# Layernorm results turned features first by transposing DMAs of 16-bit halves, in a transformer tower with routed experts on one core

## The chip, the cores and the metric

The kernel runs on 1 core of one Trainium2 chip. The metric is the device time of one execution in microseconds; the kernel before took 2347.92 us, the median of 3 runs (2347.41 to 2347.99).

The engines are TensorE (PE, with its weight loads PEld), VectorE (DVE), ScalarE (ACT), GpSimd (POOL) and SyncE (SP), which issues most DMAs. Each engine works through its own list of instructions in order and waits for others at semaphores.

## The reference, cut to what matters

The input is cut into patches, Fourier transformed along the patch and embedded: 16384 tokens of D = 256 features, in 4 sequences. Then one layer follows, in float32:

```python
h  = tok(x)                                   # (4, 4096, 256)
z  = layernorm(h)                             # no gain, no bias
a  = layernorm(z) * ln1_g + ln1_b
q, k, v = a@Wq.T + bq, a@Wk.T + bk, a@Wv.T + bv
z1 = z + q * scan(mem = decay*mem + k*v)      # along the sequence
m  = layernorm(z1) * ln2_g + ln2_b
h  = h + z1 + relu(m@W1.T + b1)@W2.T + b2     # hidden size 1024
t  = layernorm(h)
top 2 of 8 experts per token from softmax(t @ router_w.T), weights made to sum to 1
out = h + t + sum over the two experts of weight * (gelu(t@w1[e] + b1[e]) @ w2[e] + b2[e])
```

## The kernel before

The tokens are taken in NB = 32 blocks of BLK = 512 (TT = 4 groups of 128 tokens). Layernorms need tokens on the partitions ("tokens first": a tile of 128 x 4 x 256), matmuls that contract over features need the features there ("features first": 128 x 2 x 512, since D is KD = 2 groups of 128). So three times a block a layernorm's result is turned. `to_features` (L213) does it with eight PE transposes of 128 x 128 (L217) into two PSUM tiles, and ACT brings each to SBUF: with gain and bias of the layernorm as the factors of an activation (L225), or as a plain copy (L219). The three uses are

- `features1` (L291): `zz` to `hT`, for the attention's q, k and v (`retention`, L295). With `scan=True` the tokens are put in the order of the sequence while ACT copies.
- `features2` (L339): the second `zz` to another `hT`, for the hidden layer (`mlp_in`, L343, eight parts m = 0 to 7; `mlp_out`, L349, two halves).
- `features3` (L388): `tok` to `tokT`, for the router (`logits`, L392, one call for 128 tokens). `choose` (L404) then finds the two experts on DVE, and `place` (L458) counts tokens with PE and DVE and writes each token to its two experts' lists in DRAM (`xbuf`) by eight indirect DMAs from POOL (L479). What is written is `row`, made in `mlp_out`: each token's 256 values as two planes of 16-bit halves, all upper halves and then all lower ones (two ACT copies, L376), and its number (an iota on POOL, L381).

`take` (L525) finds which lists hold full tiles of 256 tokens (four more a block in steady state) and adds them to `tiles`. A slot runs one `expert_step` (L728) if more than 3 tiles wait: it issues the loads of a tile up to four ahead on SP (weights L589, the tokens L596, their shares L599), copies the next tile on ACT (`turn`, L602), and lets PE enter one tile and leave the one before (L608, L625), after which DVE makes `y` (L639 to L646) and POOL adds it to the output with two indirect DMAs (L650). The tokens of a tile already come in features first by a transposing DMA from DRAM: the DMA transposes 2-byte elements, so the planes of halves are turned (`xh`, 256 KB), and two ACT copies put the halves of each float32 together again (L606).

The order on PE, DVE, ACT and SP is that of the program (`tc.manual_schedule`, L752); POOL's is left to the scheduler. Iteration i of the main loop works on three blocks: the new one (embedding, first layernorms, attention), the middle one (hidden layer) and the old one (routing). On PE a steady iteration is: embed part 0 (L262); features2 of the middle block; embed part 1 (L273); features3 of the old; embed part 2; a slot; mlp_in 0 to 3, each followed by one `logits`; a slot and `choose`; mlp_in 4 to 6; features1 of the new; mlp_in 7; `place` and `take`; retention; a slot; mlp_out(0); the residual's transposes (L327); a slot; mlp_out(1). The iterations 0 to 3 have no slot, 4 and 5 only the last two; after the loop's last iteration, which has no new block, the last block's experts are run densely between the remaining tiles. The layernorms' `rstd` is made on POOL (L195 to L200) between its indirect DMAs, and DVE applies it (L204).

Of the kernel before, what the change touches and what calls it, by code (L numbers as in the profile page):

```python
# [12 lines left out]
F32 = mybir.dt.float32  # L13
I32 = mybir.dt.int32
U16 = mybir.dt.uint16
AF = mybir.ActivationFunctionType
ALU = mybir.AluOpType
AX = mybir.AxisListType

P = 128  # L20
# [6 lines left out]
BQ, BK, BV, DEC, G1, B1, G2, B2, MB1, EB1 = 0, 2, 4, 6, 8, 10, 12, 14, 16, 24  # L27
# [3 lines left out]
def vit_tower_kernel(  # L31
# [15 lines left out]
    nc = tc.nc  # L47
    B, NBLK, _, XW = x.shape
    D = wtok.shape[1]
# [3 lines left out]
    KD, KH = D // P, H // P  # L53
    J = STRIDE // 2
    TT = 4
    BLK = TT * P
    U = TT // 2
# [8 lines left out]
    NB = B * NBLK  # L66
    NTOK = NB * BLK
    RW = D + 4
    FIRST, DIFF, SECOND, NUMBER = D, D + 1, D + 2, D + 3


    NS = NB - 1
# [12 lines left out]
    def load_x(i):  # L85
        xb = xpool.tile([P, XW], F32, name="xb")
        nc.sync.dma_start(out=xb, in_=x[i // NBLK, i % NBLK])
        return xb
# [5 lines left out]
    with tc.tile_pool(name="prep", bufs=1) as prep:  # L94
# [4 lines left out]
        for h in range(2):  # L99
            rows = slice(h * C, (h + 1) * C)  # L100
# [21 lines left out]
    vec = const.tile([P, vecs.shape[1]], F32)  # L122
    nc.sync.dma_start(out=vec, in_=vecs)
    wqkv_sb = const.tile([P, 3, KD, D], F32)
    nc.sync.dma_start(out=wqkv_sb, in_=wqkv.rearrange("w (k p) d -> p w k d", p=P))
    w1_sb = const.tile([P, KD, H], F32)
# [41 lines left out]
    one = ctx.enter_context(tc.tile_pool(name="one", bufs=1))  # L168
    two = ctx.enter_context(tc.tile_pool(name="two", bufs=2))
# [7 lines left out]
    p_tm = ctx.enter_context(tc.tile_pool(name="p_tm", bufs=3, space=bass.MemoryType.PSUM))  # L177
    p_sm = ctx.enter_context(tc.tile_pool(name="p_sm", bufs=1, space=bass.MemoryType.PSUM))

    class Norm:  # L180


# [27 lines left out]
                    ALU.mult,  # L210
                )

    def to_features(dst, src, g=None, b=None, scan=False):  # L213
        for k in range(KD):
            ps = p_mm.tile([P, BLK], F32, name="mm")
            for t in range(TT):
                nc.tensor.transpose(ps[:, ts(t, P)], src[:, t, ts(k, P)], ident)  # L217
            if g is None:
                nc.scalar.copy(dst[:, k, :], ps)  # L219
            else:  # L220
                into = dst[:, k, :]
                if scan:
                    into = into.rearrange("p (u q r) -> p u r q", u=U, r=2)
                    ps = ps.rearrange("p (u r q) -> p u r q", u=U, r=2)
                nc.scalar.activation(  # L225
                    into, ps, AF.Identity, bias=vec[:, b + k : b + k + 1], scale=vec[:, g + k : g + k + 1]
                )

    def feature_mm(w, rhs, m):

# [7 lines left out]
    class Block:  # L238
# [14 lines left out]
        def embed(self):  # L253
# [34 lines left out]
            norm.apply(self.zz, self.h, 1)  # L288
            norm.apply(self.z, self.h, 0)

        def features1(self):  # L291
            self.hT = two.tile([P, KD, BLK], F32, name="hT")
            to_features(self.hT, self.zz, G1, B1, scan=True)

        def retention(self, m):  # L295
            if m == 0:
# [24 lines left out]
        def residual(self):  # L321
# [14 lines left out]
            nc.vector.tensor_tensor(self.h, self.h, self.z, ALU.add)  # L336
            nc.vector.tensor_tensor(self.h, self.h, mb2_sb.unsqueeze(1).to_broadcast([P, TT, D]), ALU.add)

        def features2(self):  # L339
            self.hT = two.tile([P, KD, BLK], F32, name="hT")  # L340
            to_features(self.hT, self.zz, G2, B2)

        def mlp_in(self, m):  # L343
            if m == 0:
# [4 lines left out]
        def mlp_out(self, u):  # L349
            if u == 0:  # L350
                self.norm = Norm()
            ps = p_tm.tile([P, 2, D], F32, name="tm")
            for i in range(2):
                for k in range(KH):
                    nc.tensor.matmul(  # L355
                        ps[:, i, :],
                        lhsT=self.aT[:, k, ts(u * 2 + i, P)],
                        rhs=w2_sb[:, k, :],
                        start=k == 0,
                        stop=k == KH - 1,  # L360
                    )
            nc.vector.tensor_tensor(self.h[:, ts(u, 2), :], ps, self.h[:, ts(u, 2), :], ALU.add)  # L362
            for i in range(2):
                self.norm.stats(self.h, u * 2 + i)
            if u == U - 1:
                self.norm.factors()
                self.tok = one.tile([P, TT, D], F32, name="tok")
                self.norm.apply(self.tok, self.h)
                nc.vector.tensor_tensor(self.h, self.h, self.tok, ALU.add)
                if self.i == NS:  # L370
                    return

                self.row = two.tile([P, TT, RW], I32, name="row")
                halves = self.tok.rearrange("p t d -> p (t d)").bitcast(U16).rearrange("p (t d i) -> p t d i", t=TT, i=2)
                for i in range(2):
                    nc.scalar.copy(self.row.bitcast(U16)[:, :, i * D : (i + 1) * D], halves[:, :, :, 1 - i])  # L376

                to = out[ts(self.i, BLK), :].rearrange("(u q r) d -> q u (r d)", q=P, r=2)
                self.stored = nc.sync.dma_start(out=to, in_=self.h.rearrange("p (u r) d -> p u (r d)", r=2))
                unordered("sums", self.stored, ())  # L380
                nc.gpsimd.iota(  # L381
                    self.row[:, :, NUMBER : NUMBER + 1],
                    pattern=[[2 * P, U], [1, 2]],
                    base=self.i * BLK,
                    channel_multiplier=2,
                )

        def features3(self):  # L388
            self.tokT = one.tile([P, KD, BLK], F32, name="tokT")
            to_features(self.tokT, self.tok)  # L390
# [126 lines left out]
    def unordered(name, what, others):  # L517

        tc.declare_no_dep(what.ins, group=name, keep=[o.ins for o in others], reason="rows of their own")
        after(what, others)  # L520
        tc.add_to_no_dep_group(name, what.ins)
# [201 lines left out]
    def advance(what, upto):  # L723
        while at[what] < min(upto, len(tiles)):
            getattr(tiles[at[what]], what)()
            at[what] += 1

    def expert_step():  # L728

        n = at["enter"]  # L730
        advance("load", n + AHEAD)
        advance("turn", n + 2)
        advance("enter", n + 1)
        advance("leave", n)
# [3 lines left out]
    blocks = [Block(i) for i in range(NB)]  # L738
# [3 lines left out]
    def slot():  # L742
        if len(tiles) - at["enter"] > LEFT:
            expert_step()
# [7 lines left out]
    with tc.manual_schedule(engines=MANUAL):  # L752
        xs[1] = load_x(1)
        blocks[0].differences(xs.pop(0))
        for i in range(NB + 1):
            new = blocks[i] if i < NB else None
            mid = blocks[i - 1] if i >= 1 else None
            old = blocks[i - 2] if i >= 2 else None
            embed = new.embed() if new else iter(())
            next(embed, None)  # L760
            if mid:
                mid.features2()
            next(embed, None)
            if old:
                old.features3()
            next(embed, None)
            slot()
            for m in range(KH):
                if mid:
                    mid.mlp_in(m)  # L770
                if old and m < TT:
                    old.logits(m)
                if m == TT - 1:
                    slot()
                    if old:
                        old.choose()
                if new and m == KH - 2:
                    new.features1()
                if not new and m == KH - 3:
                    take(old.i + 1, old, old.place())  # L780
            if old and new:
                take(old.i + 1, old, old.place())
            if i + 1 < NB:
                blocks[i + 1].differences(xs.pop(i + 1))
                if i + 2 < NB:
                    xs[i + 2] = load_x(i + 2)
            if new:
                for m in range(KD):
                    new.retention(m)
            slot()  # L790
            if mid:
                mid.mlp_out(0)
            if new:
                new.residual()
            slot()
            if mid:
                mid.mlp_out(1)

        last = blocks[NS]
        for e in range(E):  # L800
            tiles.insert(len(tiles) - 2 * (E - 1 - e), Expert(e, last))
        expert_step()
        expert_step()
        last.features3()
        for t in range(TT):
            last.logits(t)
        last.choose()
        last.combine()
        while at["leave"] < len(tiles):
            expert_step()  # L810
# [82 lines left out]
```

## Time and profile before

| what | value |
|---|---|
| median of 3 runs | 2347.92 us (2347.41 to 2347.99) |
| profiled execution | 2348.05 us, its span 2346.0 us, mean granted PE clock 0.987 |
| DMA, all kinds | 255.91 MB, mean 109 GB/s |
| DMA queue of SP | 30.9% of 16 engines' span |
| DMA queue of POOL | 16.3% |
| longest waits of PE | 25.9 us for `wsum` at the start, 8.7 us for `xd`, 6.5 us for `zz` (2 times), 6.0 us for `xT` (2), 5.7 us for `tok` (1) |

A timeline row has the start in the span, the time to the end of the last instruction of the row, engine, line, operation, output and inputs, and in brackets how long the engine had been idle and what released it. A group row of the page has count, busy time and mean duration (ns) of one, then idle time before its instructions. Matmul ends are modelled, so consecutive PE rows overlap a little, and the step from one start to the next is the better cost. A float32 matmul is two records.

### The profile page before, as it was taken

The page shows a single profiled execution, that of the slowest core. Times are in us where ns is not written, and L with a number is a line of the kernel's source. Part 1 is how long each engine was busy: PE and PEld are TensorE (multiplying, and loading weights), DVE is VectorE, ACT ScalarE, POOL GpSimd, SP SyncE. Part 2 cuts the span into 40 slices and gives each one's busy share as a digit, 9 for nine tenths or more (in the row PEclk, how much of TensorE's full clock was granted, in tenths as well). Part 3 has the DMA queues.
Part 4 walks back from the last instruction along what each step waited for, and adds up shares of the span by engine and source line. Part 5 has one row for each costly group of instructions (what it writes and reads, how often), then busy time and mean ns, then how long its engine had stood idle before and what let it go on. Part 6 is the DMA issues. An engine that isn't in the chain of part 4 may idle for free. (4 is left out here: it accounts for less than half of the span.)

```text
span 2346.0 us, 28985 instructions
## 1 busy us (share of the span) xinstructions
PE 2253.9 (96%) x9324; PEld 1646.0 (70%) x9324; DVE 1364.3 (58%) x4112; ACT 708.0 (30%) x1149; POOL 935.5 (40%) x828
## 2 busy tenths in 40 slices
PE   3999999999999999999999999999999999998994
PEld 2577677777777777777777777777777777776773
DVE  6466656556666565665656556655565665654442
ACT  0122323332223333222233232323333222333331
POOL 0022334344444433444444344444433444444334
PEclk8999999999999999999999999999999999999997
DMA  5021334554445444544454544445455544444994
GB/s 146 19 82 46 113 98 102 111 111 104 109 102 123 111 109 107 121 90 112 113 124 103 104 119 100 114 102 123 104 114 109 113 98 102 105 105 110 195 202 88
DMA packets 264488, 255.91 MB, mean 109 GB/s; under 512 B 186128, under 2 KB 224144, under 8 KB 260240
## 3 DMA queue, kind: packets, MB, share of 16 engines
q1 hardware_dynamic: 214560, 186.41, 30.9%
q0 software_dynamic: 49632, 67.39, 16.3%
q8 instruction: 74, 1.21, 0.2%
q14 instruction: 78, 0.64, 0.1%
q10 hardware_dynamic: 144, 0.26, 0.0%
HBM read 131.26 MB, written 88.39 MB: 94 GB/s over the span
## 5 line engine op out<-in xcount | busy, mean ns | idle before, releaser
L650 POOL DMA_INDIRECT out<-y,xg x262 | 416.0, 1588 | 608.9 <-DVE y L646 313.2
L233 PE MATMUL mm<-hT,w_sb 128*128 128x512 f32 x1024 | 478.3, 600 | 0.0
L355 PE MATMUL tm<-w_sb,aT 128*128 128x256 f32 x2048 | 452.8, 379 | 0.0
L355 PEld LDWEIGHTS tm<-w_sb,aT 128*128 128x128 f32 x2048 | 388.9, 190 | 54.1 <-issue 1.4
L479 POOL DMA_INDIRECT xbuf<-row,to x248 | 329.6, 1329 | 188.8 <-DVE full L537 111.2
L233 PE MATMUL mm<-hT,wqkv_sb 128*128 128x512 f32 x768 | 338.0, 596 | 0.1
L233 PEld LDWEIGHTS mm<-hT,w_sb 128*128 128x128 f32 x1024 | 184.7, 190 | 158.0 <-issue 154.2
L347 ACT ACTIVATE aT<-mm,vec 128x512 f32<-128x512 f32 x256 | 175.9, 687 | 386.5 <-PE mm L233 386.5
L195 POOL TENSOR_SCALAR rstd<-mv 128x4 f32<-128x4 f32 x96 | 38.7, 403 | 570.7 <-DVE mv L189 570.7
L233 PEld LDWEIGHTS mm<-hT,wqkv_sb 128*128 128x128 f32 x768 | 143.9, 191 | 169.6 <-issue 153.8
L613 PE MATMUL mm<-xT,w 128*128 128x256 f32 x1048 | 254.5, 386 | 7.4 <-ACT xT L606 6.0
L630 PE MATMUL tm<-w,ge 128*128 128x256 f32 x1048 | 249.4, 381 | 1.1 <-issue 0.6
L273 PE MATMUL tm<-weff,xd 128*128 128x256 f32 x1024 | 233.2, 381 | 8.7 <-DVE xd L250 8.7
L621 ACT ACTIVATE ge<-mm,w 128x256 f32<-128x256 f32 x262 | 109.7, 469 | 406.8 <-issue 390.5
L644 DVE TENSOR_TENSOR y<-tm,w 128x512 f32<-128x512 f32 x131 | 90.6, 691 | 242.3 <-PE tm L630 210.3
L613 PEld LDWEIGHTS mm<-xT,w 128*128 128x128 f32 x1048 | 197.6, 193 | 45.8 <-issue 13.9
L630 PEld LDWEIGHTS tm<-w,ge 128*128 128x128 f32 x1048 | 200.0, 191 | 33.1 <-issue 5.9
L273 PEld LDWEIGHTS tm<-weff,xd 128*128 128x128 f32 x1024 | 191.0, 191 | 32.8 <-DVE xd L250 9.1
L376 ACT COPY row<-tok 128x1024 uint16<-128x1024 uint16 x62 | 61.8, 1043 | 496.9 <-issue 376.0
L606 ACT COPY xT<-xh 128x512 uint16<-128x512 uint16 x262 | 182.1, 767 | 44.9 <-DMA xh<-xbuf 44.8
L362 DVE TENSOR_TENSOR h<-tm,h 128x512 f32<-128x512 f32 x64 | 44.0, 687 | 181.5 <-PE tm L355 172.2
L262 PE MATMUL tm<-wsum,xb 128*128 128x256 f32 x512 | 118.2, 385 | 25.9 <-ACT wsum L118 25.9
(128 smaller groups left out, 2336.1 us busy)
## 6 DMA issues: line engine op xcount, KB each, us to landing
w<-in_wex SPq DMA_DIRECT2D x139, 641.5 KB
xb<-in_x SPq DMA_DIRECT2D x32, 1040.0 KB
out<-h SPq DMA_DIRECT2D x31, 512.0 KB
out<-y,xg POOLq DMA_INDIRECT x262
xbuf<-row,to POOLq DMA_INDIRECT x248
xh<-xbuf SPq DMA_TRANSPOSE x131
xg<-xbuf SPq DMA_DIRECT2D x131, 4.0 KB
xbuf<-none SPq DMA_DIRECT2D x8, 260.0 KB
```

The costliest lines, as they stand in the source:

```text
L233: nc.tensor.matmul(ps, lhsT=w[:, k, ts(m, P)], rhs=rhs[:, k, :], start=k == 0, stop=k == KD - 1)
L262: nc.tensor.matmul(ps[:, u, :], lhsT=od[:, j, ts(u, P)], rhs=wsum[:, j, :], start=j == 0, stop=j == J - 1)
L273: nc.tensor.matmul(ps[:, i, :], lhsT=xd[:, i, j, ts(u, P)], rhs=weff[:, i * J + j, :], start=j == 0, stop=j == J - 1,)
L347: nc.scalar.activation(self.aT[:, m, :], ps, AF.Relu, bias=vec[:, MB1 + m : MB1 + m + 1])
L355: nc.tensor.matmul(ps[:, i, :], lhsT=self.aT[:, k, ts(u * 2 + i, P)], rhs=w2_sb[:, k, :], start=k == 0, stop=k == KH - 1,)
L479: write = nc.gpsimd.indirect_dma_start(out=xbuf, out_offset=bass.IndirectOffsetOnAxis(ap=to[:, c, t : t + 1], axis=0), in_=self.row[:, t, ...
L606: nc.scalar.copy(halves[:, :, :, 1 - i], self.xh[:, i * KD : (i + 1) * KD, :])
L613: nc.tensor.matmul(ps[:, m, :], lhsT=self.w[:, k * D + m * P : k * D + (m + 1) * P], rhs=self.xT[:, k, :], start=k == 0, stop=k == KD - 1,)
L621: nc.scalar.activation(self.ge[:, m, :], ps[:, m, :], AF.Gelu, bias=self.w[:, 5 * D + m : 5 * D + m + 1])
L630: nc.tensor.matmul(ps[:, c, :], lhsT=self.ge[:, k, ts(c, P)], rhs=w[:, (2 + k) * D : (3 + k) * D], start=k == 0, stop=k == KD - 1,)
L644: nc.vector.tensor_tensor(y, ps, w[:, 4 * D : 5 * D].unsqueeze(1).to_broadcast([P, 2, D]), ALU.add)
L650: add = nc.gpsimd.indirect_dma_start(out=out, out_offset=bass.IndirectOffsetOnAxis(ap=self.xg[:, c, NUMBER - D : NUMBER - D + 1], axis=0), ...
```

## The change

At the start, gain and bias of both layernorms are folded into the weights that follow them: 12 and 16 matmuls of one column give W times bias, DVE adds it to the biases in `vec`, and four ACT multiplications scale the rows of the weights by the gain.

`features1` and `features2` use a new class `Turn`. `split` makes two planes of 16-bit halves of `zz` with two ACT copies, `start` issues one transposing DMA from SBUF to SBUF on SP (512 KB), and `join` puts the halves into `hT` with four ACT copies. For the router, `row`, which holds such planes anyway, is moved from `mlp_out` to a method of its own (`rows`) in the next iteration, and is turned by four DMAs of 128 KB (`turn3`), joined into `tokT` by four DVE copies (`join3`). There is one buffer `planes` and one buffer `turned` for all uses. `logits` come one `mlp_in` later, and the slot and `choose` with them. The last iteration, without a new block, is written out by itself: there features3 is still done on PE (as it is for the last block), and the routing of the block before the last stands ahead of most of the last hidden layer, behind two slots.

```diff
+    for w, g, b, to, n in ((wqkv_sb, G1, B1, BQ, 3 * KD), (w1_sb, G2, B2, MB1, KH)):
+        w4 = w if n == 3 * KD else w.unsqueeze(1)
+        ps = p_sm.tile([P, KH], F32, name="sm")
+        for c in range(n):
+            i, m = (c // KD, c % KD) if n == 3 * KD else (0, c)
+            for k in range(KD):
+                nc.tensor.matmul(
+                    ps[:, c : c + 1],
+                    lhsT=w4[:, i, k, ts(m, P)],
+                    rhs=vec[:, b + k : b + k + 1],
...
+        nc.vector.tensor_tensor(vec[:, to : to + n], vec[:, to : to + n], ps[:, :n], ALU.add)
+        for k in range(KD):
+            nc.scalar.mul(w4[:, :, k, :], w4[:, :, k, :], vec[:, g + k : g + k + 1])
...
+    def halves(a):
+        return [a.bitcast(U16)[:, :, i : 2 * D : 2] for i in (1, 0)]
+    class Turn:
+        def split(self, src):
+            planes = one.tile([P, TT, 2 * D], U16, name="planes")
+            for i, half in enumerate(halves(src)):
+                nc.scalar.copy(planes[:, :, i * D : (i + 1) * D], half)
+            self.start([planes.rearrange("p t d -> p (t d)")])
+        def start(self, planes):
+            self.turned = one.tile([P, TT, 2, KD, P], U16, name="turned")
+            n = TT // len(planes)
+            for j, plane in enumerate(planes):
+                to = self.turned[:, j * n : (j + 1) * n]
+                nc.sync.dma_start(out=to.rearrange("p t i k q -> p (t i k) q"), in_=plane, transpose=True)
+        def join(self, dst, copy, scan=False):
+            for k in range(KD):
+                to = dst[:, k, :].bitcast(U16)
+                for i in range(2):
+                    if scan:
...
+                    else:
+                        to_i = to.rearrange("p (t q i) -> p i t q", t=TT, i=2)[:, 1 - i]
+                        src = self.turned[:, :, i, k, :]
+                    copy(to_i, src)
...
+        def split1(self):
+            self.turn = Turn()
+            self.turn.split(self.zz)
         def features1(self):
             self.hT = two.tile([P, KD, BLK], F32, name="hT")
-            to_features(self.hT, self.zz, G1, B1, scan=True)
+            self.turn.join(self.hT, nc.scalar.copy, scan=True)
...
+        def turn3(self):
+            self.turn = Turn()
+            self.turn.start([self.row.bitcast(U16)[:, t, : 2 * D] for t in range(TT)])
+        def join3(self):
+            self.tokT = one.tile([P, KD, BLK], F32, name="tokT")
+            self.turn.join(self.tokT, nc.vector.tensor_copy)
```

The main loop after the change (the last block's experts follow as before):

```python
        for i in range(NB):
...
            embed = new.embed()
            next(embed)
            if mid:
                mid.features2()
            if old:
                old.rows()
                old.turn3()
            next(embed)
            next(embed, None)
            slot()
            if old:
                old.join3()
            for m in range(KH):
                if mid:
                    mid.mlp_in(m)
                if m == 1:
                    new.split1()
                if old and 1 <= m <= TT:
                    old.logits(m - 1)
                if m == TT:
                    slot()
                    if old:
                        old.choose()
                if m == KH - 2:
                    new.features1()
...
            new.residual()
            slot()
            new.split2()
            if mid:
                mid.mlp_out(1)
        last, old = blocks[NS], blocks[NS - 1]
        last.features2()
        old.rows()
        slot()
        slot()
        old.features3()
        for t in range(TT):
            old.logits(t)
        for m in range(KH):
            last.mlp_in(m)
            if m == 0:
                old.choose()
            if m == 2:
                take(NS, old, old.place())
            if m == TT:
                expert_step()
        last.mlp_out(0)
        expert_step()
        last.mlp_out(1)
```

More of the change, by code (lines that the diff above doesn't have):

```diff
@@ L178, in vit_tower_kernel @@
     p_sm = ctx.enter_context(tc.tile_pool(name="p_sm", bufs=1, space=bass.MemoryType.PSUM))
+    for w, g, b, to, n in ((wqkv_sb, G1, B1, BQ, 3 * KD), (w1_sb, G2, B2, MB1, KH)):
[8 more added lines that the diff above has]
+                    rhs=vec[:, b + k : b + k + 1],
+                    start=k == 0,
+                    stop=k == KD - 1,
+                )
+        nc.vector.tensor_tensor(vec[:, to : to + n], vec[:, to : to + n], ps[:, :n], ALU.add)
+        for k in range(KD):
+            nc.scalar.mul(w4[:, :, k, :], w4[:, :, k, :], vec[:, g + k : g + k + 1])
     class Norm:
@@ L211, in apply, with to_features @@
                 )
-    def to_features(dst, src, g=None, b=None, scan=False):
+    def to_features(dst, src):
         for k in range(KD):
@@ L217, in to_features @@
                 nc.tensor.transpose(ps[:, ts(t, P)], src[:, t, ts(k, P)], ident)
[L218 to L227, printed above, removed]
+            nc.scalar.copy(dst[:, k, :], ps)
+    def halves(a):
[17 more added lines that the diff above has]
+                    if scan:
+                        to_i = to.rearrange("p (u q r i) -> p i u r q", u=U, r=2, i=2)[:, 1 - i]
+                        src = self.turned[:, :, i, k, :].rearrange("p (u r) q -> p u r q", r=2)
+                    else:
+                        to_i = to.rearrange("p (t q i) -> p i t q", t=TT, i=2)[:, 1 - i]
+                        src = self.turned[:, :, i, k, :]
+                    copy(to_i, src)
     def feature_mm(w, rhs, m):
@@ L337, in residual, with split2 @@
             nc.vector.tensor_tensor(self.h, self.h, mb2_sb.unsqueeze(1).to_broadcast([P, TT, D]), ALU.add)
+        def split2(self):
+            self.turn = Turn()
+            self.turn.split(self.zz)
         def features2(self):
             self.hT = two.tile([P, KD, BLK], F32, name="hT")
-            to_features(self.hT, self.zz, G2, B2)
+            self.turn.join(self.hT, nc.scalar.copy)
         def mlp_in(self, m):
@@ L371, in mlp_out @@
                     return
[L373 to L376, printed above, removed]
                 to = out[ts(self.i, BLK), :].rearrange("(u q r) d -> q u (r d)", q=P, r=2)
@@ L380, in mlp_out, with rows @@
                 unordered("sums", self.stored, ())
[L381 to L386, printed above, removed]
+        def rows(self):
+            self.row = two.tile([P, TT, RW], I32, name="row")
+            for i, half in enumerate(halves(self.tok)):
+                nc.scalar.copy(self.row.bitcast(U16)[:, :, i * D : (i + 1) * D], half)
+            nc.gpsimd.iota(
+                self.row[:, :, NUMBER : NUMBER + 1],
+                pattern=[[2 * P, U], [1, 2]],
+                base=self.i * BLK,
+                channel_multiplier=2,
+            )
+        def turn3(self):
+            self.turn = Turn()
+            self.turn.start([self.row.bitcast(U16)[:, t, : 2 * D] for t in range(TT)])
+        def join3(self):
+            self.tokT = one.tile([P, KD, BLK], F32, name="tokT")
+            self.turn.join(self.tokT, nc.vector.tensor_copy)
         def features3(self):
@@ L754, in vit_tower_kernel @@
         blocks[0].differences(xs.pop(0))
-        for i in range(NB + 1):
-            new = blocks[i] if i < NB else None
+        for i in range(NB):
+            new = blocks[i]
             mid = blocks[i - 1] if i >= 1 else None
             old = blocks[i - 2] if i >= 2 else None
-            embed = new.embed() if new else iter(())
-            next(embed, None)
+            embed = new.embed()
+            next(embed)
             if mid:
                 mid.features2()
-            next(embed, None)
             if old:
-                old.features3()
+                old.rows()
+                old.turn3()
+            next(embed)
             next(embed, None)
             slot()
+            if old:
+                old.join3()
             for m in range(KH):
@@ L770, in vit_tower_kernel @@
                     mid.mlp_in(m)
-                if old and m < TT:
-                    old.logits(m)
-                if m == TT - 1:
+                if m == 1:
[3 more added lines that the diff above has]
+                if m == TT:
                     slot()
@@ L776, in vit_tower_kernel @@
                         old.choose()
-                if new and m == KH - 2:
+                if m == KH - 2:
                     new.features1()
-                if not new and m == KH - 3:
-                    take(old.i + 1, old, old.place())
-            if old and new:
+            if old:
                 take(old.i + 1, old, old.place())
@@ L786, in vit_tower_kernel @@
                     xs[i + 2] = load_x(i + 2)
-            if new:
-                for m in range(KD):
-                    new.retention(m)
+            for m in range(KD):
+                new.retention(m)
             slot()
@@ L792, in vit_tower_kernel @@
                 mid.mlp_out(0)
-            if new:
-                new.residual()
+            new.residual()
             slot()
+            new.split2()
             if mid:
                 mid.mlp_out(1)
-        last = blocks[NS]
+        last, old = blocks[NS], blocks[NS - 1]
+        last.features2()
+        old.rows()
+        slot()
+        slot()
+        old.features3()
+        for t in range(TT):
+            old.logits(t)
+        for m in range(KH):
+            last.mlp_in(m)
+            if m == 0:
+                old.choose()
+            if m == 2:
+                take(NS, old, old.place())
+            if m == TT:
+                expert_step()
+        last.mlp_out(0)
+        expert_step()
+        last.mlp_out(1)
         for e in range(E):
```

## The prediction

> **What bounds the kernel now.** I read the page's busy shares first, then TensorE (PE) in order of time over one block in mid run, then VectorE (DVE) over the same stretch, because the question is which engine would be late if PE had less to do.
>
> ```profile
> span 2346.0 us, 28985 instructions
> PE 2253.9 (96%) x9324; PEld 1646.0 (70%) x9324; DVE 1364.3 (58%) x4112; ACT 708.0 (30%) x1149; POOL 935.5 (40%) x828
> PEclk8999999999999999999999999999999999999997
> ```
>
> PE is busy 96% at nearly full granted clock: its own work is the bound. Now PE's timeline (start, us, line, operation, idle before it) over part of one block:
>
> ```profile
> 1226.90 1.11 PE L327 MATMUL tm<-ident,ret 128*128 128x128 f32 x8
> 1231.31 7.07 PE L355 MATMUL tm<-w_sb,aT 128*128 128x256 f32 x32
> 1238.22 3.62 PE L262 MATMUL tm<-wsum,xb 128*128 128x256 f32 x16
> 1241.67 1.04 PE L217 MATMUL mm<-ident,zz 128*128 128x128 f32 x8
> 1242.54 3.62 PE L273 MATMUL tm<-weff,xd 128*128 128x256 f32 x16
> 1246.00 1.04 PE L217 MATMUL mm<-ident,tok 128*128 128x128 f32 x8
> 1253.78 1.88 PE L233 MATMUL mm<-hT,w_sb 128*128 128x512 f32 x4
> ```
>
> No gap stands between rows, so a row's cost is the step to the next start: eight transposes cost 1242.54 - 1241.67 = 0.87 us, 109 ns each. The same L217 row at 1203.21 and 1271.04 gives the block's period, 67.83 us. DVE in the same stretch:
>
> ```profile
> 1244.46 1.39 DVE L204 TENSOR_SCALAR tok<-h,mv,rstd 128x256 f32<-128x256 f32 x4 [3.21 <-POOL rstd L200]
> 1245.88 1.23 DVE L369 TENSOR_TENSOR h<-h,tok 128x1024 f32<-128x1024 f32 x1
> 1254.79 1.38 DVE L204 TENSOR_SCALAR zz<-h,mv,rstd 128x256 f32<-128x256 f32 x4 [2.36 <-POOL rstd L200]
> 1256.08 1.38 DVE L204 TENSOR_SCALAR z<-h,mv,rstd 128x256 f32<-128x256 f32 x4
> 1258.46 0.62 DVE L646 TENSOR_SCALAR y<-y,tile_share 128x256 f32<-128x256 f32 x2
> ```
>
> DVE is 58% busy, yet here it runs some 3 us behind the PE work it serves. Today that is harmless: after `tok` the routing logits need PE and ACT only.
>
> **What goes.** Of 96 sets of eight transposes with their PSUM copies, the change keeps two (the last two blocks' features3). 94 x 0.87 = 82 us of PE; 2.61 us per block in steady state. Whether that is kept is decided by when each replacement arrives. I count from R, the end of the residual's transposes (1228.0 above), with the new PE order: slot 3.45, mlp_out(1) 6.91, embed 3.45 + 6.91, slot 3.45, then mlp_in at 1.72 each. mlp_in(0) is due at R+24.2, the first logits (now after mlp_in(1)) at R+27.6.
>
> **Prices of the parts.** The halves' copies and the turning transfers have near rows:
>
> ```profile
> L606 ACT COPY xT<-xh 128x512 uint16<-128x512 uint16 x262 | 182.1, 767 | 44.9 <-DMA xh<-xbuf 44.8
> L376 ACT COPY row<-tok 128x1024 uint16<-128x1024 uint16 x62 | 61.8, 1043 | 496.9 <-issue 376.0
> 278.97 1.28 SPq L596 DMA_TRANSPOSE xh<-xbuf  x1
> 282.12 1.38 ACT L606 COPY xT<-xh 128x512 uint16<-128x512 uint16 x2 [12.20 <-DMA xh<-xbuf]
> 283.55 3.50 PE L613 MATMUL mm<-xT,w 128*128 128x256 f32 x8 [2.62 <-ACT xT L606]
> ```
>
> A split is two copies like L376's, 2.0 us. A join on ACT is four like L606's (182.1/262 = 0.70): 2.8 us. A 256 KB transfer from DRAM takes 1.28 us on SP and reaches its reader 3.15 us after issue. The new ones read SBUF, which no row shows, and move 512 KB: at least 3.15 us, at most (everything doubled) 6.3; I take 5.0, the issue once and the rest doubled. The routed block's turn is four issues of 128 KB: 4 x 1.28 on SP plus about 1.9 after the last, 7.0 us. DVE's join has no row: 0.31 us a copy if it ran like L646's 256 elements, 0.61 at half of L369's 1024; I take 0.60, as 512 elements are nearest to that row, so 2.4 us.
>
> The Trainium skill (VectorE: DVE Perf Modes, The three transpose paths) speaks against the change: 390 ns for TensorE's 128x128 transpose, 1309 ns for the DMA crossbar's. The trace has 109 ns sustained and 3.15 us / 8 = 394 ns a block. If sixteen blocks a turn cost the page's figure in sequence, a turn would last 21 us, all three joins would be late, and my estimate would be near 3400 us.
>
> **Second features (turn 2), hidden.** `zz` is done at R+7.4, split R+9.5, landed R+14.5, joined R+17.3, due R+24.2: 6.9 us spare. SP had issued the slot's loads by R+3.4. Behind the waiting join on ACT stand the row copies and the slot's xT and Gelu, needed no sooner.
>
> **Routing (turn 3), late on DVE.** `tok` is done at 1245.85 = R+17.9; rows (2.0, now behind join 2) R+20.0; landed about R+27. DVE reaches the join later still. In program order: h+tok until R+19.1; two embed additions with statistics, 1.89 each (1248.43 to 1250.32), R+22.9; POOL's rstd 2.36, R+25.3; zz and z 2.67, R+28.0; the slot's share and y 1.65, R+29.6. (The 1.33 us that DVE spent waiting for `ms` behind the row copies is gone and counted so.) Four copies: first half of the features R+30.8, second R+32.0. PE waits 3.2 us and, after one 0.18 matmul, 1.0 more: **4.2 us per block** where it waited for nothing.
>
> **Clock.** The 283.55 row shows it: after 2.62 us of idleness eight matmuls took 3.50 instead of 1.89. After an idle time of 1.72 us at 73.7 the granted clock from 76 to 79 us was still 1.00, so a bound of zero stands. I take 1.3 us, between 0 and 1.8, near the 1.6 of that row. The skill (TensorE: Matmul & The Clock Gate, Part 1) wants an idle window of about 3.4 us before the clock halves; by that rule many of these waits would cost nothing extra and the sum would be nearer 2430; the 2.62 us row already contradicts it.
>
> **First features (turn 1), a little late.** SP may issue it only when join 3 has emptied the one `turned` buffer, R+32.0; landed R+37; needed after the relu of mlp_in(6), about R+46: hidden. But ACT's join takes 2.8 where two PSUM copies took 1.5. From mlp_in(6)'s end X, relu ends X+0.8, joins X+2.2 and X+3.6; PE, after mlp_in(7), placement (0.36) and one 0.87 matmul, waits from X+3.1: **0.5 us**. Choosing moves one mlp_in later; it ends 4.4 us after its slot, PE wants it after 5.2.
>
> **Sum.** Steady block: -2.6 + 4.2 + 1.3 + 0.5 = +3.4; blocks 6 to 31 have all four slots, 26 x 3.4 = +88. Blocks 2 to 5 lack the slot before mlp_in, so logits are due at R+20.7, while rows are done about R+19, landed R+26 and joined R+28.4: 7.7 us late, and -2.6 + 7.7 + 1.3 + 0.5 = +6.9 each, +28. Start: block 0's retention waits for zz (55.3) + 2.0 + 5.0 + 1.4 = 63.7 instead of 56.7, block 1 nets +1: +8. Folding 28 pairs of one-column matmuls and four weight multiplies lies under PE's first waits (25.9 and 8.7 us); uncovered it would cost 5. Tail: PE idled 5.65, 1.42, 0.88, 2.02 and 3.35 us after 2120; now the second of the two slots waits for xT behind the row copies (tok 7.6 us after mlp_out(1), +2.0 +1.4, where PE arrives at 3.5), but the last routing is ready some 7 us earlier: -4, between -12 and +6. The ending scatter-adds shift with PE. Total 88 + 28 + 8 - 4 = **+120**: span 2466, and with the 2.05 us around it (profiled execution 2348.05) **2468 us**; that execution is within 0.13 us of the median of the runs, 2347.92, so nothing is to convert.
>
> **Rivals.** (a) *The gain is kept*, the faster side: DVE finishes join 3 by R+27.6, or the wait stays under the 2.6 us removed. It needs DVE 4.4 us earlier than its rows allow; ACT and SP have the spare time, DVE is idle 42%. Then 2348 - 82 + 8 = 2274 us. Against: z, zz and y stand ahead in program order, and even copies of 0.31 us leave 2.6 + 0.4 us. Chance 0.10; just landing within 0.2%, about what a measurement can tell from no change, 0.02. (b) *SBUF-sourced turns are slow.* Turn 3's cover is R+20 to R+29.6; from 9.6 us for the four on, each further us costs 30 blocks one. At 13 us: 2468 + 30 x 3.4 = 2570. Against: 7.0 by rows. The transfers also stand in SP's queue ahead of expert loads, but those run four tiles ahead. Chance 0.20. (c) Forecast, 0.68; its own range: copies at 0.31 us (-30), no clock loss (-38), tail -8 give 2392; clock 1.8 (+15), turns doubled early in the run (+20), tail +10 give 2513. The range adds the nearer part of (b): 2390 to 2540.
>
> **What will show it.** Right: PE idle about 4 us once a block before the logits, released by DVE's copies into tokT; DVE itself never waiting for the turn's DMA in mid run; half-clock stretches each block; period near 71.3 us. Wrong: a period near 65.2 (a); DVE or ACT idle on the turn's DMA (b); PE waiting for hT or xT instead.

## The result and the profile after

The changed kernel takes 2549.06 us (median of 4 runs, 2547.7 to 2550.7) against 2347.95 for the kernel before (4 runs): a ratio of 1.0857 with a 95% interval of 1.0838 to 1.0875. The prediction was 2468 us, 2390 to 2540: the direction was right, the loss was 201 us instead of 120, and the time lies above the range.

From the page of the profile after: span, busy time, clock row, and the groups of the splits and of ACT's joins.

```profile
span 2545.6 us, 28277 instructions
...
PE 2294.2 (90%) x8628; PEld 1616.4 (63%) x8628; DVE 1403.5 (55%) x4234; ACT 944.3 (37%) x1349; POOL 940.2 (37%) x828
...
PEclk8899999999999999999999999999999999999997
...
L268 ACT COPY hT<-turned 128x512 uint16<-128x512 uint16 x256 | 235.7, 1070 | 23.1 <-DMA turned<-planes 23.0
...
L248 ACT COPY planes<-zz 128x1024 uint16<-128x1024 uint16 x128 | 127.2, 1042 | 217.5 <-DVE zz L222 217.5
```

PE executes 696 records fewer, and yet its busy time rose from 2253.9 to 2294.2 us: the same matmuls ran longer. And it is idle 250 us. The waits of PE say for what (engine, line, released by; us in total, times, longest):

```profile
PE sm L454 <- DVE tokT L268: 91.6, 56, 5.7
PE mm L274 <- ACT hT L268: 87.0, 65, 14.7
PE sm L187 <- DMA wqkv_sb<-in_wqkv: 19.6, 1, 19.6
```

The first line was forecast. The second, nearly as large, was forecast at 0.5 us a block; from 500 to 2240 us it is 52.8 us in 24 blocks, 2.2 each. One block of PE's timeline, where the kernel before had no gap at all:

```profile
1307.05 3.60 PE L274 MATMUL mm<-hT,w_sb 128*128 128x512 f32 x8
1313.10 0.39 PE L454 MATMUL sm<-rw_sb,tokT 128*128 128x8 f32 x2 [2.46 <-DVE tokT L268]
1313.77 0.39 PE L454 MATMUL sm<-rw_sb,tokT 128*128 128x8 f32 x2 [0.28 <-DVE tokT L268]
1314.01 2.62 PE L274 MATMUL mm<-hT,w_sb 128*128 128x512 f32 x4
1317.13 2.69 PE L274 MATMUL mm<-hT,w_sb 128*128 128x512 f32 x4
...
1332.45 1.13 PE L274 MATMUL mm<-hT,wqkv_sb 128*128 128x512 f32 x2 [1.05 <-ACT hT L268]
1334.72 5.85 PE L274 MATMUL mm<-hT,wqkv_sb 128*128 128x512 f32 x13 [1.15 <-ACT hT L268]
```

The two rows of four records after the logits take 2.62 and 2.69 us where the same row took 1.88 in the kernel before: PE ran at half clock for part of the time (mean granted clock 0.72 from 1314 to 1320 us, 1.00 from 1320 to 1324). What released PE stands in the timelines of DVE and of ACT (same columns: start, duration, engine, line, operation, tiles, count, and the idle time before it). DVE's, around the logits:

```profile
1311.73 0.62 DVE L704 TENSOR_SCALAR y<-y,tile_share 128x256 f32<-128x256 f32 x2
1312.26 1.46 DVE L268 COPY tokT<-turned 128x512 uint16<-128x512 uint16 x4
```

ACT's, with both joins of the block:

```profile
1297.37 2.63 ACT L268 COPY hT<-turned 128x512 uint16<-128x512 uint16 x4
...
1329.94 4.73 ACT L268 COPY hT<-turned 128x512 uint16<-128x512 uint16 x4
```

DVE begins the join the moment it has done `y`, as forecast, and is quick (0.37 us a copy). Of ACT's two joins, the one without reordering (second features) takes 2.63 us, the one that puts tokens in the sequence's order 4.73. In the stretch from 500 to 2240 us ACT's joins waited for turning transfers 0.4 us in all, and DVE's not at all.

The period of a block, from one residual's last transpose to the next, read from the trace: 67.83 us before, alternating between about 72.5 and 74.4 after, 73.6 in the mean of blocks 6 to 31. Where the 200 us are (spans, 2345.96 to 2545.61):

| stretch | before | after | difference | predicted |
|---|---|---|---|---|
| start, to the end of block 1's residual | 116.9 | 135.9 | +19.0 | +8 |
| blocks 2 to 5 | 229.4 | 263.0 | +33.6 | +28 |
| blocks 6 to 31, 26 of them | 1763.5 | 1914.7 | +151.2, 5.8 a block | +88, 3.4 a block |
| after the last residual | 236.2 | 231.9 | -4.3 | -4 |

### The profile page after: what moved, and what is told of

Its sections match the earlier page's. It is cut to its first block, busy times and chain, and to the rows that moved or that the text cites. A ratio compares the mean times of both kernels' runs of the same rounds, so it can differ in the third digit from the quotient of the medians.

```text
span 2545.6 us, 28277 instructions
## 1 busy us (share of the span) xinstructions
PE 2294.2 (90%) x8628; PEld 1616.4 (63%) x8628; DVE 1403.5 (55%) x4234; ACT 944.3 (37%) x1349; POOL 940.2 (37%) x828
## 5 line engine op out<-in xcount | busy, mean ns | idle before, releaser
L274 PE MATMUL mm<-hT,w_sb 128*128 128x512 f32 x1024 | 516.6, 646 | 3.5 <-ACT hT L268 3.5
L274 PE MATMUL mm<-hT,wqkv_sb 128*128 128x512 f32 x768 | 382.3, 652 | 83.5 <-ACT hT L268 83.5
L274 PEld LDWEIGHTS mm<-hT,wqkv_sb 128*128 128x128 f32 x768 | 153.8, 207 | 290.0 <-issue 174.7
L274 PEld LDWEIGHTS mm<-hT,w_sb 128*128 128x128 f32 x1024 | 200.3, 204 | 191.5 <-issue 183.7
L268 ACT COPY hT<-turned 128x512 uint16<-128x512 uint16 x256 | 235.7, 1070 | 23.1 <-DMA turned<-planes 23.0
L314 PE MATMUL tm<-weff,xd 128*128 128x256 f32 x1024 | 228.0, 381 | 1.4 <-DVE xd L291 1.4
L248 ACT COPY planes<-zz 128x1024 uint16<-128x1024 uint16 x128 | 127.2, 1042 | 217.5 <-DVE zz L222 217.5
L454 PEld LDWEIGHTS sm<-rw_sb,tokT 128*128 128x128 f32 x512 | 89.3, 220 | 177.4 <-DVE tokT L268 119.4
```

The costliest lines, as they stand in the source:

```text
L248: nc.scalar.copy(planes[:, :, i * D : (i + 1) * D], half)
L268: copy(to_i, src)
L274: nc.tensor.matmul(ps, lhsT=w[:, k, ts(m, P)], rhs=rhs[:, k, :], start=k == 0, stop=k == KD - 1)
L314: nc.tensor.matmul(ps[:, i, :], lhsT=xd[:, i, j, ts(u, P)], rhs=weff[:, i * J + j, :], start=j == 0, stop=j == J - 1,)
```

## The experiments

Theory W: the loss is PE's new waits (for DVE's join before the logits, for ACT's join before the attention) and the half clock that follows them. Rival C: the load of the added transfers and copies slows the work beside it. Rival F: the folding costs something in every block. Theories P and Q, later, are about what makes the clock halve. Unless a ratio is given, a number is one run of the experiment; the kernel before took 2350.79 and 2349.97 us beside the first and the second four.

**k1_fold.** The kernel before with the folding and plain copies out of PSUM.

```diff
-            to_features(self.hT, self.zz, G1, B1, scan=True)
+            to_features(self.hT, self.zz, scan=True)
-            to_features(self.hT, self.zz, G2, B2)
+            to_features(self.hT, self.zz)
```

> The kernel before with the folding of gain and bias alone; all turns stay on PE. Theory W (PE's new waits and the half clock after each of them make the loss): only the start grows, by the 4.7 us that the second embed matmuls start later in the changed kernel (45.39 instead of 40.64 us): about 2353 us. Theory C (the added transfers and copies slow other work, by load): the same, nothing is added in the blocks. Theory F (the folding costs something in every block): well above 2360.

Measured: 2352.68 us. Block 0's residual ends at 75.3 instead of 70.3 us, and a steady block takes 67.83 as before. Rival F falls by the period; the folding costs 5 us once, which the prediction had taken as hidden.

**k5_carry.** The same, plus all splits and all turning transfers at about their places; what they bring is not read.

```diff
+                if new and m == 1:
+                    new.carry1()      # split zz, turn the planes
...
+                if new:
+                    old.carry3()      # turn row
...
+            if new:
+                new.carry1()          # split the second zz, turn the planes
```

> The folded kernel with all turns on PE, which also makes all splits and issues all the turning transfers of the change at about its places, but nobody reads what they bring (no joins). W: the load alone costs nothing, as the folded kernel within 0.5%, about 2353 us. C: the load is the cause, so most of the 200 us come back: above 2450.

Measured: 2353.44 us, 67.83 us a block. Its page shows that the load was there:

```profile
DMA packets 462892, 305.25 MB, mean 130 GB/s; under 512 B 384528, under 2 KB 422544, under 8 KB 458640
```

The kernel before moved 255.91 MB in 198 thousand packets fewer. As far as transfers and splits go, rival C is refuted: 49 MB of transposing transfers and 127 us of splits on ACT cost 0.8 us beside k1_fold, one run of each, and nothing in the period. The joins are not in this kernel; k8_both, below, carries them all at 65.8 us a block.

**k2_turn2.** The folding, and of the turns only that of the second features by DMA.

```diff
+            if new:
+                new.split2()
...
-            to_features(self.hT, self.zz)      # in features2
+            self.turn.join(self.hT, nc.scalar.copy)
```

> The folding, and of the three turns only that of the second features by DMA. W: this turn has 6.9 us to spare, so each steady block loses 0.87 us of PE and nothing is late: some 2353 - 28 x 0.87 + 3 in the first blocks = 2332 us, faster than before. C: a third of the added load and so about a third of the loss, near 2415 us.

Measured: 2345.39 us, 7.3 less than k1_fold where some 21 were expected. C's sign is wrong, and W's amount: a block takes 67.43, 0.4 less and not 0.87. PE's timeline and then DVE's show where the rest is:

```profile
1246.42 1.54 PE L234 MATMUL mm<-ident,tok 128*128 128x128 f32 x8
1247.80 1.46 PE L317 MATMUL tm<-weff,xd 128*128 128x256 f32 x6
```

```profile
1245.76 1.38 DVE L221 TENSOR_SCALAR tok<-h,mv,rstd 128x256 f32<-128x256 f32 x4 [3.21 <-POOL rstd L217]
```

The eight transposes of `tok` now take 1.38 us from their start to the next one's instead of 0.87: PE comes 0.87 us sooner, while DVE is still applying `tok`. A saving ahead of a wait is partly spent in it.

**k3_noscan.** The changed kernel without the reordering.

```diff
-            self.turn.join(self.hT, nc.scalar.copy, scan=True)
+            self.turn.join(self.hT, nc.scalar.copy)
```

> The changed kernel, with the first features joined in the order in which they came (the reordering along the sequence is left out, so attention works on tokens in another order). The four copies should take 2.6 us as those of the second features do, instead of 4.7. W: PE's two waits of 1.05 and 1.14 us before the attention shrink to one of 0.5; with the half clock that follows them 2549 - 30 x (1.7 + 1.7) = 2447 us; if the half clock has another cause, 2549 - 30 x 1.7 = 2498. C: the load is the same, 2549 less at most a few us.

Measured: 2459.98 us, near W's 2447. From its page:

```profile
L268 ACT COPY hT<-turned 128x512 uint16<-128x512 uint16 x256 | 168.0, 758 | 27.3 <-DMA turned<-planes 27.3
```

256 copies take 168.0 us instead of 235.7: 0.66 each with a step of 4 bytes between the halves written, and 1.18 (4.73/4) with the reordering's step of 8. The reordering, in half of the copies, is 68 us of ACT's time, none of which PE would see if it did not wait for these joins. From 500 to 2240 us PE no longer waits for `hT` at all. This kernel leaves out the order of the sequence, so its results are other ones.

**k6_join1.** The same wait attacked from the other side: ACT joins as slowly, but earlier.

```diff
                 if m == TT:
+                    new.features1()
                     slot()
...
-                if m == KH - 2:
-                    new.features1()
```

> The changed kernel with the join of the first features two parts of the hidden layer earlier on ACT (after mlp_in(4) instead of 6). W: the two waits before the attention (2.2 us) and their half clock (1.7) go, PE's wait for the logits stays: 2549 - 30 x 3.9 = 2432 us. C: no change, 2549.

Measured: 2458.68 us: the attention's wait is gone, but 90 us are gained where 117 were expected. The reason stands behind the wait that is left:

```profile
1261.11 0.39 PE L454 MATMUL sm<-rw_sb,tokT 128*128 128x8 f32 x2 [2.46 <-DVE tokT L268]
...
1262.23 3.76 PE L274 MATMUL mm<-hT,w_sb 128*128 128x512 f32 x4
...
1266.49 2.84 PE L274 MATMUL mm<-hT,w_sb 128*128 128x512 f32 x4
```

3.76 us for a row that takes 1.88 at full clock: the half clock after the logits' wait stayed. In the trace's clock records from 400 to 2000 us it is 106 us here, 116 us in the changed kernel.

**k7_join3.** The other wait attacked: DVE joins before it applies `z` and before the slot's `y`.

```diff
             norm.apply(self.zz, self.h, 1)
+            yield
             norm.apply(self.z, self.h, 0)
...
             next(embed)
+            next(embed)
+            if old:
+                old.join3()
             next(embed, None)
             slot()
-            if old:
-                old.join3()
```

> The changed kernel with DVE's join for the router put ahead of the application of z and of the slot's y. W: DVE then waits for the transfer, until about 27 us after the residual's transposes; the logits wait about 0.9 us instead of 2.7, without half clock: 2549 - 30 x (1.8 + 1.7) = 2444 us. C: 2549. If the transfers of the routed block take longer than 7 us, DVE is held and less is gained.

Measured: 2415.26 us, 29 better than expected. From 500 to 2240 us PE waits for the logits 6.6 us instead of 66.3. The attention's waits are as before, but now hardly any half clock follows (7 us from 400 to 2000 us):

```profile
1263.86 1.12 PE L274 MATMUL mm<-hT,wqkv_sb 128*128 128x512 f32 x2 [1.05 <-ACT hT L268]
1266.14 9.28 PE L274 MATMUL mm<-hT,wqkv_sb 128*128 128x512 f32 x21 [1.15 <-ACT hT L268]
```

9.28 us for 21 records is full speed (0.44 each, as 10.55 for 24 in k1_fold). W's rule "each wait has its half clock" does not hold as it was put.

**k4_fill.** PE is given useless matmuls where it waits.

```diff
+                if old and m == 1:
+                    fill(3, mid.hT)
                 if old and 1 <= m <= TT:
                     old.logits(m - 1)
...
+            if mid:
+                fill(2, mid.hT)
             for m in range(KD):
                 new.retention(m)
```

> The changed kernel with useless matmuls (128x512) where PE waits: three before the first logits, 2.6 us, and two before the attention, 1.7 us. They compute nothing that is used. W: PE stays busy, the half clock goes, and the kernel gets faster by doing more: 30 x 3.4 us less, about 2450 us, if all of the half clock comes from the waits. If the clock does not follow PE's idleness: 2549 or up to 20 more. C: 2549 or more.

Measured: 2487.06 us: PE does some 31 x 4.3 us more work and the kernel is 62 us faster. No half clock is left in the records from 400 to 2000 us. That it stops short of 2450 is the filler's own wait, for the PSUM buffer it shares with the placement:

```profile
1367.70 0.53 PE L526 MATMUL sm<-both,rc 128*128 128x32 f32 x4
1369.40 1.96 PE L282 MATMUL sm<-hT,ident 128*128 128x512 f32 x4 [1.17 <-DVE before L532]
1371.19 5.31 PE L274 MATMUL mm<-hT,wqkv_sb 128*128 128x512 f32 x12
```

The attention's 12 records after the filler take 5.31 us, 0.44 each: full speed. So the half clock does follow PE's idleness, and it is no fixed property of these matmuls. The filler's own waits of up to 1.2 us, one a block, never brought it.

**k9_phase.** k7_join3 with one useless matmul a block, in a place where PE is busy.

```diff
             new.split2()
+            if i >= 6:
+                fill(1, mid.hT)
```

> The kernel k7_join3 (only the two short waits before the attention left, 68.25 us a block, which is 20.0 stretches of 3.41 us) with one useless matmul of 128x512 a block where PE is busy, from block 6 on: 0.87 us, so that a block is no whole number of such stretches. Theory P (the half clock is decided over fixed stretches of 3.41 us, so it depends on where in them a wait falls): half-clock stretches come back in some blocks, the time is above 2415 + 26 x 0.87 = 2438 by 10 us or more. Theory Q (waits of 1.2 and 1.4 us with work between them never halve the clock): 2438 and no half clock in mid run.

Measured: 2439.9 us. That is Q's time, but it does not speak against P: compared with k7_join3, the logits' wait went from 6.6 to 0.5 us (from 500 to 2240 us), and the stretch after the last residual is 5.5 us shorter (229.5 for 235.0), which together hide the half clock. The clock is P's: the periods are 68.97 in some blocks and 70.67 in others, with 31 us of half clock from 400 to 2000 us, after the same pair of waits. Two blocks, one without and one with it:

```profile
1069.69 1.13 PE L274 MATMUL mm<-hT,wqkv_sb 128*128 128x512 f32 x2 [1.05 <-ACT hT L268]
1071.97 9.71 PE L274 MATMUL mm<-hT,wqkv_sb 128*128 128x512 f32 x22 [1.15 <-ACT hT L268]
...
1138.67 1.12 PE L274 MATMUL mm<-hT,wqkv_sb 128*128 128x512 f32 x2 [1.05 <-ACT hT L268]
1140.95 11.41 PE L274 MATMUL mm<-hT,wqkv_sb 128*128 128x512 f32 x22 [1.16 <-ACT hT L268]
```

The same waits, to 0.02 us, cost 1.7 us of clock or nothing. The clock records show why. In each of the traces all changes of the granted clock lie whole multiples of 3.413 us apart, so there is a fixed grid of such stretches. Here are the stretches around the two pairs of waits (from, to, length, PE busy, granted clock, then DMA):

```profile
1066.16:1069.58 3.42, 2.48 (x9) 1.00 0.96 304
1069.58:1072.99 3.41, 2.15 (x5) 1.00 0.41 50
1072.99:1076.40 3.41, 3.41 (x10) 1.00 0.22 78
1134.43:1137.85 3.42, 3.19 (x11) 1.00 0.93 311
1137.85:1141.26 3.41, 1.43 (x3) 1.00 0.34 38
1141.26:1144.67 3.41, 3.41 (x5) 0.50 0.31 84
```

In the first block the two waits lie in two stretches, and the clock stays full. In the second most of both lies in one stretch, PE is idle 2.0 us of it, and the next stretch runs at half clock. From 400 to 2000 us of this run the clock halved after all nine stretches with more than 1.8 us of idle PE and after none with less than 1.7. Over the same stretch of time in all traces it halved 83 times, always after a stretch with at least 1.36 us of idle PE, and it did not halve after some stretches with up to 2.02 us, so idle time in the stretch is not the whole rule. The trace of k7_join3 fits too: its period of 68.25 us is 20.0 stretches, and from block to block its pair of waits stays on two sides of a stretch's end; only in the two blocks where both fell mostly into one stretch did half clock follow, the 7 us above.

**k8_both.** Both moves, of k6 and k7.

> Both moves. W: a steady block loses 2.2 + 1.8 + 3.4 us of its 73.6: 66.2, and the whole 2549 - 30 x 7.4 = 2327 us, below the kernel before. C: 2549.

Measured: 2331.32 us, and in a later job (k8_timed) with 4 runs 2334.03, a ratio of 0.992 to the kernel before (0.9903 to 0.9938).

> k8_both again, timed against the kernel before: 2331 us, a ratio of 0.993.

Most steady blocks take 65.5 to 66.1 us, 65.8 in the mean; 67.83 less the transposes' 2.61 would be 65.2. In steady state the change now keeps 2.1 of the 2.6 us that it takes from PE. What is lost still is at the start: block 4's residual ends at 316.5 us instead of 280.9 in the kernel before.

**k10_best.** So PE turns as before until block 6, and the two foldings are put into block 0, behind its embedding and in front of its attention.

```diff
+    START = 6
...
+            if self.i < START:
+                to_features(self.hT, self.zz, scan=True)
+                return
...
+            if i == 0:
+                fold(wqkv_sb, G1, B1, BQ, 3 * KD)
...
+            if i == 0:
+                fold(w1_sb, G2, B2, MB1, KH)
```

> k8_both with PE turning as before until block 6, where the slots begin to fill the iteration, and the folding put where PE waits in block 0 anyway. Waits-and-clock theory: start and blocks 1 to 5 as in the kernel before, 26 blocks at 65.7 instead of 67.83, tail -3: 2348 - 55 - 3 = 2290 us. If part of the early loss is not from the early turns, up to 2310.

Measured: 2300.21 us (4 runs), a ratio of 0.978 (0.9764 to 0.9797): faster than both kernels, 10 us above what was expected. Its page:

```profile
span 2298.5 us, 28390 instructions
...
PE 2205.2 (96%) x8748; PEld 1594.8 (69%) x8748; DVE 1396.8 (61%) x4218; ACT 894.8 (39%) x1313; POOL 936.7 (41%) x828
```

And PE's waits, the longest of them at the very start, for the embedding's first operand (25.89 us in the kernel before):

```profile
PE tm L307 <- ACT wsum L118: 25.8, 1, 25.8
PE mm L682 <- ACT xT L675: 14.9, 4, 7.4
...
PE sm L465 <- DVE tokT L272: 5.5, 20, 0.7
```

PE is at 96% again, with 49 us less to do, and blocks 6 to 31 take 65.7 us each, as expected. The 10 us are at the start, where block 0's residual still ends at 79.7 instead of 70.3 us: the second folding holds PE for 6.85 us in front of the first attention, whose 24 records then take 13.19 us instead of 11.15.

## Why the prediction was right in direction and too low

**Late on DVE: mechanism right, size too large.** The step said that DVE reaches the router's join behind z, zz and y, at R+29.6; it did at R+29.2 (1312.26, R being 1283.04). The size failed in the copy: 0.37 us and not 0.60. In steps between starts the waits cost 3.1 us and not 4.2 (2.62 before the first pair of records, 0.49 before the second). k7 confirms the order as the cause.

**First features, "a little late", 0.5 us: the failed step.** The wait and its place in the order were foreseen, its size was not. The prediction counted four copies at 0.70 us each, the price of the `xT` row, and overlooked that with `scan` the halves are written 8 bytes apart, not 4. They took 1.18 each; in steps the two waits are 1.21 and 1.40, 2.6 us a block where 0.5 was charged. The kernel before gave no warning: ACT's copies of 4-byte values out of PSUM take about as long with the reordering (first row) as without it (second row).

```profile
1203.99 1.49 ACT L225 ACTIVATE hT<-mm,vec 128x512 f32<-128x512 f32 x2
1248.30 1.45 ACT L225 ACTIVATE hT<-mm,vec 128x512 f32<-128x512 f32 x2
```

k3 and k6 both take the wait away. Whether the larger step alone makes the 2-byte copy slow, or also the reordered pattern around it, no run separates.

**Clock, 1.3 us: the other term that was too small.** The records have 116 us of half clock from 400 to 2000 us, 5.3 us and so 2.7 us lost in each of 21.7 blocks. k4 shows that it belongs to the waits, k6 and k7 that most of it is the logits' wait, and k9 that a pair of waits of 1.1 us costs 1.7 us or nothing by where it falls. A price "per wait" was the wrong form: what counts is how much idle time falls into one stretch of the grid. The rule weighed beside it, that only an idle stretch of about 3.4 us halves the clock, is not what these runs show: no wait for the logits or for `hT` in mid run was longer than 2.8 us. That the stretches are fixed in time is also what the Trainium skill says (TensorE: Matmul & The Clock Gate, Part 1: the window is free-running, 3413 ns). It agrees with k9 and with the lengths in the clock records, where 45 of the changed kernel's 55 half-clock stretches last 3.41 us and nine of the others twice or four times that.

Put together for a steady block: -2.6 + 3.1 + 2.6 + 2.7 = +5.8, as measured; predicted -2.6 + 4.2 + 0.5 + 1.3 = +3.4. The copy on DVE, priced too high, hid part of the other two errors. Over 26 blocks the 2.4 us make 63 of the 81 us by which the forecast was short.

**Start: +8 became +19.** Folding was called hidden: k1 measured 5.0 us. In block 0 the first half of the join with reordering takes 2.4 us where 1.4 was counted. Block 1 lost 5.3 us where 1 was counted: PE waits 3.55 us for the second features there, and runs at half clock after it (0.50 from 97 to 101 us). Blocks 2 to 5, +28 predicted and +33.6 measured, were right in kind: their logits waited 5.7, 5.0, 4.9 and 4.3 us, where 7.7 were counted, but the attention's waits and the half clock took more than that difference.

**Turns hidden: right.** A 512 KB turn in block 0, where nothing covers it, took 4.5 us from split to join (ACT waited 4.49), against 5.0 taken; the four of `row` 7.0 us from first issue to DVE's join in block 2 (154.59 to 161.62), against 7.0. That refutes rival (b), slow turns from SBUF. The Trainium skill's 1309 ns for a crossbar transpose of 128x128 (VectorE: DVE Perf Modes, The three transpose paths) is not what each block of a larger transfer costs here: 4.5 us for 16 blocks is 280 ns each. Rival (a), the gain kept, is not what the change did, but k8 shows that its condition was the right one: with the join earlier on DVE (and ACT's as well) most of the gain appears in steady state.

**Tail: right** in the sum, -4.3 for -4; its parts were not taken apart by a run.

## What to carry to other kernels

When work is moved off the busiest engine, its replacement must be timed to the place in the order where the result is read: this change was sound in its loads, and lost 200 us mainly because two joins stood too late in two other engines' lists; moving them forward brought 218 us (2549.06 to 2331.32). Price a strided copy by a row with the same stride and the same element size. And count a wait of the matmul engine higher than its length: in the changed kernel 5.7 us of waits a block brought 2.7 us of half clock on top, and in k9_phase the same pair of waits brought 1.7 us or nothing, by where it fell.

## What the runs showed of the hardware that was not expected

- An ACT copy of 128x512 16-bit elements takes 0.66 us when it writes every second element and 1.18 us when it writes every fourth, in the reordered pattern; DVE takes 0.37 us for the first kind.
- Useless matmuls in PE's waits made a kernel 62 us faster (2549.06 to 2487.06), since the granted clock stayed full from 400 to 2000 us where the changed kernel had 116 us of half clock.
- 49 MB more of 256-byte transposing packets (30.9% to 42.1% of the DMA engines' time on that queue in k5_carry) made the kernel 0.8 us slower, one run of each, and left the period of a block at 67.83 us.
- The granted clock changes only on a fixed grid of 3.413 us. From 400 to 2000 us it never halved after a stretch with less than 1.36 us of idle PE, and a pair of waits of 1.05 and 1.15 us halved it only where most of both fell into one stretch.
